# A spiking recurrence and its score matrix: the last step reordered, and three split fetches put back whole

## The chip, the core and the metric

The kernel runs on one core of a Trainium2 chip. The metric is the device time of one execution in microseconds (us); less is better. The core has TensorE (PE in the profile, with its weight loads as PEld), VectorE (DVE), ScalarE (ACT), GpSimd (POOL) and SyncE (SP), a main on-chip memory (SBUF), accumulators (PSUM, eight banks) and 16 DMA engines that move data between them and the chip's memory.

## The reference

B = 1024 sequences of T = 50 item numbers pick rows of a table of N = 100001 items with D = 128 values (row 0 counts as zero). Running means over the sequence are normalised over the batch and drive a leaky neuron per sequence and value; the mean number of its spikes is multiplied with the whole table.

```
e = emb[seq]                                   # (1024, 50, 128)
prefix = jnp.cumsum(e, axis=1)
uF = prefix / minimum(t_idx, lengths)
y = (uF - mean) * rsqrt(var + eps) * gamma + beta   # mean, var over the batch, for each step
for each of the 50 steps t:
    v = v + (y[t] - v) / 2
    spike = v >= 1
    v = v - spike
uF_out = mean of the spikes over the steps     # (1024, 128)
scores = uF_out @ emb.T                        # (1024, 100001), float32
```

The result is 409.6 MB, the table 51 MB.

## The kernel before, in words

The kernel has two stages, and its order of instructions on each engine is the order of the code (`manual_schedule`); waits between engines follow from the tiles that they read and write.

**First stage: the recurrence.** At the start SP fetches the first 40 blocks of the table (a block is 1024 items, `HALF`; 98 blocks in all) into SBUF as rows. Then come 50 steps in the loop over `t`. For each step GpSimd gathers 8 times 128 table rows by an indirect DMA (L218, tile `e`, pool `gp` with two buffers), two steps ahead. TensorE transposes each 128 x 128 piece and adds it to the running sums in PSUM (`pre[0]` and `pre[1]`, one bank each, L332). VectorE divides by the lengths (`uF`, L341, in two halves), takes the statistics (L342, L348), ScalarE and VectorE make the scale `a`, ScalarE writes the scaled input (`x`, L382) into a PSUM tile `vt` (tags `v0` and `v1` in turn), and VectorE adds minus half of `negv` (`step`, L385). `spiked` (L311) adds the spikes of v to `count`; `over` (L304) lets ScalarE write v - 1 as bfloat16 into `d`; `rest` (L308) makes `negv` = spike - v of it, for the next step.

**The last step** (t = 49) is cut so that the second stage can begin early. Its columns go in three pieces: A (128 sequences), B (512) and C (384). Before the sums of this step, VectorE runs `spiked` and `rest` on all 1024 columns of the last v, and makes `near` of A's columns. A is finished on VectorE alone (`vA`, `countA`). PE fills its idle time with 16 transposes of the identity into a tile `warm` (L417) that lies in the bank pair `v0`, where the last v is. Then TensorE multiplies the first two blocks of the table with `countA` (`firsts`: two tiles `po0`, `po1`, each in two halves of 512), and ScalarE (three) and VectorE (one) evict the halves, scaled by 1/T, into `o0` (in a gather tile, tag `e`) and `o1` (tag `rlen` in pool `once`), each half stored by itself (`first_store`, L433 and L435). `x`, `step` and `spiked` of B and C stand between them.

**Second stage: the product.** For each block of the table TensorE transposes the rows, ScalarE and VectorE split the result into two parts (`prepare`, L163 and L164), and TensorE multiplies both parts with the eight groups of counts (`product`, L171) into PSUM tiles of two banks (pool `psum`, four tiles, where the first stage's banks were). The blocks go in groups of `WIDTHS`: four groups of 2, four of 3, thirteen of 6. For each group, and each n of 8 groups of sequences, the blocks' PSUM tiles are evicted by VectorE (L513) and ScalarE (L515) in turn, as `turn` is even or odd, into one output tile, which SP stores in one DMA (`store`, L180): 3 MB for a group of 6. In the groups of 2 there are four output tiles, in a pool that takes the place in SBUF which `once` and the other first-stage pools had; later there are three. The pools are opened with `reuse_waits="tile"`: a new tile waits for what used its place.

**Fetches in the second stage.** From the ninth group on, two times in a group, ScalarE's queue fetches three more blocks (`fetch`, L106 to L139) in one DMA. For the blocks q = 43, 61 and 79 (`LOW`) this is split: the third of the three blocks is fetched by three DMAs of 123, 3 and 2 rows of 4 KB (L116), ahead of one DMA for the other two blocks (L120). Each DMA, of SP and of ScalarE, is given one of eight semaphores in turn, and a DMA on a semaphore is issued when the one before it on that semaphore has landed.

Of the kernel before, what the change touches and what calls it, by code (L numbers as in the profile page):

```python
# [35 lines left out]
NARROW, MIDDLE = 4, 8  # L36
LOW = (43, 61, 79)


@with_exitstack  # L40
def rec_kernel(
# [62 lines left out]
    def fetch(r, k, q, n):  # L104
# [3 lines left out]
        whole = n - (size(q + n - 1) < HALF)  # L108
        if q in LOW:
            whole -= 1  # L110
            n = whole
            one = r[:, k + whole, :]
            src = table[(q + whole) * HALF : (q + whole + 1) * HALF, :].rearrange("(p k) d -> p (k d)", k=KQ)
            p0 = 0
            for pw in (123, 3, 2):
                engine.dma_start(out=one[p0 : p0 + pw, :], in_=src[p0 : p0 + pw, :])  # L116
                p0 += pw
            assert p0 == P
        if whole:
# [63 lines left out]
    with ExitStack() as ph:  # L183
# [122 lines left out]

        def rest(d, v):
            nc.vector.scalar_tensor_tensor(negv, d, 0.0, v, ALU.is_ge, ALU.subtract)  # L308

        def spiked(out, cs, v):  # L310
            nc.vector.scalar_tensor_tensor(out, v, V_TH, count[:, cs], ALU.is_ge, ALU.add)  # L311

        whole = slice(0, B)
        halves = [slice(h * BANK, (h + 1) * BANK) for h in range(B // BANK)]
        v = None

# [3 lines left out]
        for t in range(T):  # L320
            last = t == T - 1
            e = es.pop(t)
            if last:
                spiked(count, whole, v)
                rest(d, v)
                near = once.tile([P, P], F32, tag="r0", name="near")
                nc.vector.tensor_scalar(near, negv[:, :P], -0.5, hgb[:, 1:2], ALU.mult, ALU.add)
            uF = up.tile([P, B], F32, tag="uF", name=f"uF_{t}")
            bs = sp.tile([P, B // BANK, 6], F32, tag="bs", name=f"bs_{t}")
            for h, cs in enumerate(halves):  # L330
                for k in range(0, BANK, P):
# [7 lines left out]
                        skip_group_check=True,  # L339
                    )  # L340
                nc.vector.scalar_tensor_tensor(uF[:, cs], rlen[:, cs], 1.0 / (t + 1), pre[h], ALU.max, ALU.mult)  # L341
                nc.vector.bn_stats(bs[:, h, :], uF[:, cs])  # L342
# [19 lines left out]
            if t and not last:  # L362
                rest(d, v)

# [16 lines left out]
            def x(vt, cs):  # L381
                nc.scalar.activation(vt, uF[:, cs], AF.Identity, bias=hgb[:, 1:2], scale=a)  # L382
# [4 lines left out]
            if not last:  # L387
# [4 lines left out]
                step(vt, whole)  # L392
                v = vt
                d = over(t, v)
                if t + 2 < T:
# [18 lines left out]

        warm = vp.tile([P, HALF], F32, tag="v0", name="warm")
        for k in range(2 * KQ):
            nc.tensor.transpose(warm[:, k % KQ * P : (k % KQ + 1) * P], ident, ident)  # L417
        vC = vp.tile([P, B - BANK - P], F32, tag="v1", name="vC")
        groups = [(slice(P, P + BANK), pre[1], countB), (slice(P + BANK, B), vC, countC)]
        for cs, vt, _ in groups:  # L420
            nc.scalar.activation(uF[:, cs], uF[:, cs], AF.Identity, bias=mv[:, 0:1], scale=-1.0)

        po0 = accp.tile([P, HALF], F32, tag="po0", name="po_0_0")
        po1 = vp.tile([P, HALF], F32, tag="v0", name="po_0_1")
        o0 = gp.tile([P, HALF], F32, tag="e", name="o_0_0")
        o1 = once.tile([P, HALF], F32, tag="rlen", name="o_0_1")
        firsts = [(q, po, o, h, cs) for q, po, o in ((0, po0, o0), (1, po1, o1)) for h, cs in enumerate(halves)]
# [9 lines left out]

        for k, (cs, vt, _) in enumerate(groups):
            x(vt, cs)
            first_store(*firsts[k])  # L440
        for cs, vt, c in groups:
            step(vt, cs)
            spiked(c, cs, vt)
        for f in firsts[2:]:
            first_store(*f)


# [5 lines left out]
    opening = ExitStack()  # L453
    turn = 0
    blocks = 0
# [99 lines left out]
```

## Time and profile before

| What | us |
|---|---|
| Median of three runs (1578.18 to 1581.87) | 1579.38 |
| The profiled execution, its own time | 1581.87 |
| Its span, first to last instruction | 1579.7 |
| v of step 48 done (L385) | 503.54 |
| First product with `countA` starts | 512.16 |
| First store is issued | 514.87 |
| Last store is issued | 1561.73 |

| Engine | busy us | share of the span |
|---|---|---|
| PE | 1111.3 | 70% |
| PEld | 785.6 | 50% |
| DVE | 945.9 | 60% |
| ACT | 667.3 | 42% |
| POOL | 381.0 | 24% |

A line of the timeline has the start, the time busy, the engine, the line, the operation, the tile written and the tiles read, their shapes, and in brackets how long the engine was idle before and what released it. A line of waits has the engine that waited, for whom, the sum in us, how often, and the longest. A line of a table by stretch has the stretch, its length, the busy time of PE, PEld, DVE, ACT and POOL with the number of instructions, the granted share of TensorE's clock, the mean busy share of the 16 DMA engines, and GB/s. The granted clock's first record in this profile is at 465.03 us; ahead of it the column prints full clock.

### The profile page before, as it was taken

What the parts mean: (1) busy time and instruction counts of PE and PEld (TensorE: products, weight loads), DVE (VectorE), ACT (ScalarE), POOL (GpSimd) and SP (SyncE); (2) the same over time, 40 slices, a digit from 0 to 9 for tenths busy, and PEclk for the clock granted to TensorE, in tenths of its full rate; (3) what the DMA queues carried; (4) which work ended last, traced back from release to release, by engine and by line L of the source; (5) the groups of instructions that cost most, each with busy time, mean ns of one, the idle gap of its engine ahead of it and who ended that gap; (6) DMA issues with size and microseconds to landing.
All of it is one profiled execution on the core that took longest, in us unless ns stands there. A gap on an engine that the chain in (4) does not pass through costs nothing.

```text
span 1579.7 us, 12244 instructions
## 1 busy us (share of the span) xinstructions
PE 1111.3 (70%) x4452; PEld 785.6 (50%) x4452; DVE 945.9 (60%) x1125; ACT 667.3 (42%) x697; POOL 381.0 (24%) x406
## 2 busy tenths in 40 slices
PE   4544444444445988899887778886887868888884
PEld 2211111111122766667666566665666656666663
DVE  5777777777777656566555455554555545555552
ACT  2333333333333544555444344443444434444542
POOL 7777777777776000000000000000000000000000
PEclk9999999999995999999999999998999989999998
DMA  9711111111121899999999999998999999999998
GB/s 349 260 53 52 53 52 53 53 53 53 51 80 43 357 415 403 424 414 382 430 425 431 393 426 430 428 430 359 429 427 428 430 366 424 430 429 429 429 427 358
DMA packets 51337, 488.12 MB, mean 309 GB/s; under 512 B 10103, under 2 KB 10360, under 8 KB 30028
## 3 DMA queue, kind: packets, MB, share of 16 engines
q1 hardware_dynamic: 30752, 430.86, 64.7%
q0 software_dynamic: 12800, 26.24, 5.6%
q10 hardware_dynamic: 7724, 30.23, 5.0%
q8 instruction: 35, 0.57, 0.1%
q14 instruction: 26, 0.21, 0.0%
HBM read 77.69 MB, written 409.60 MB: 308 GB/s over the span
## 4 chain that ended last, share of the span: by engine, by line
DMA 53%; POOL 18%; PE 12%; issue 8%; ACT 5%; DVE 2%; ACTq 0%; SPq 0%; DVEq 0%; POOLq 0%
DMA scores<-o 43%; POOL e L218 18%; PE po L171 11%; DMA e<-in_L_rec_emb_table,idx 6%; ACT o L515 4%; DMA rows<-in_L_rec_emb_table 4%; DVE o L513 1%; PE pt L147 0%; ACT pairs L163 0%; PE pre L332 0%; DMA idx<-in_r_seq 0%; DVE pairs L164 0%; DVE negv L308 0%; DVE bs L342 0%; DVE uF L341 0%
## 5 line engine op out<-in xcount | busy, mean ns | idle before, releaser
L513 DVE TENSOR_SCALAR o<-po 128x1024 f32<-128x1024 f32 x391 | 464.1, 1221 | 358.4 <-DMA scores<-o 309.2
L515 ACT ACTIVATE o<-po 128x1024 f32<-128x1024 f32 (+1 forms) x391 | 389.1, 1019 | 551.9 <-DMA scores<-o 330.2
L218 POOL DMA_INDIRECT e<-in_L_rec_emb_table,idx x400 | 380.3, 951 | 123.8 <-issue 112.5
L332 PE MATMUL pre<-ident,e 128*128 128x128 f32 x400 | 179.6, 463 | 230.0 <-DMA e<-in_L_rec_emb_table,idx 229.8
L171 PE MATMUL po<-pairs,countB 128*128 128x512 f32 (+1 forms) x1120 | 289.0, 403 | 64.6 <-ACT o L515 51.7
L171 PE MATMUL po<-pairs,countC 128*128 128x512 f32 (+1 forms) x840 | 227.9, 418 | 62.4 <-ACT o L515 62.4
L171 PEld LDWEIGHTS po<-pairs,countB 128*128 128x128 f32 x1120 | 207.7, 191 | 126.8 <-ACT o L515 68.3
L332 PEld LDWEIGHTS pre<-ident,e 128*128 128x128 f32 x400 | 73.5, 184 | 339.3 <-DMA e<-in_L_rec_emb_table,idx 338.3
L171 PEld LDWEIGHTS po<-pairs,countC 128*128 128x128 f32 x840 | 163.3, 201 | 108.5 <-ACT o L515 74.2
L164 DVE TENSOR_TENSOR pairs<-pt,pairs 128x1024 fp32r<-128x1024 f32 x70 | 84.6, 1216 | 84.0 <-ACT pairs L163 84.0
L341 DVE SCALAR_TENSOR_TENSOR uF<-rlen,pre 128x512 f32<-128x512 f32 x100 | 68.3, 683 | 109.4 <-PE pre L332 109.4
L147 PE MATMUL pt<-ident,rows 128*128 128x128 f32 (+1 forms) x768 | 104.6, 281 | 10.3 <-issue 4.9
L352 ACT ACTIVATE r<-mv,eps 128x1 f32<-128x1 f32 x50 | 14.7, 295 | 225.4 <-DVE mv L348 225.4
L147 PEld LDWEIGHTS pt<-ident,rows 128*128 128x128 f32 (+1 forms) x768 | 93.5, 146 | 27.0 <-issue 10.3
L171 PE MATMUL po<-hi,countB 128*128 128x512 f32 x208 | 84.7, 407 | 16.0 <-ACT o L515 12.0
L292 PE MATMUL pre<-zT,ls 128*128 128x512 f32 x100 | 78.1, 783 | 22.7 <-DVE uF L341 18.8
L171 PE MATMUL po<-lo,countB 128*128 128x512 f32 x208 | 81.8, 393 | 0.0
L304 ACT ACTIVATE d<-v,less 128x1024 bf16<-128x1024 f32 x49 | 54.6, 1114 | 63.6 <-DVE v L385 63.6
L171 PE MATMUL po<-hi,countC 128*128 128x512 f32 x156 | 65.5, 420 | 21.8 <-ACT o L515 21.7
L163 ACT CAST pairs<-pt 128x1024 fp32r<-128x1024 f32 x70 | 70.5, 1007 | 12.6 <-PE pt L147 12.6
L171 PE MATMUL po<-pairs,countA 128*128 128x512 f32 x280 | 69.3, 394 | 7.3 <-ACT o L515 7.3
L382 ACT ACTIVATE v<-uF,hgb,a 128x1024 f32<-128x1024 f32 x49 | 59.2, 1208 | 30.6 <-DVE a L378 30.5
(85 smaller groups left out, 847.1 us busy)
## 6 DMA issues: line engine op xcount, KB each, us to landing
scores<-o SPq DMA_DIRECT2D x96, 3072.0 KB, 19.7
scores<-o SPq DMA_DIRECT2D x32, 1536.0 KB, 8.7
scores<-o SPq DMA_DIRECT2D x30, 1024.0 KB, 8.6
rows<-in_L_rec_emb_table ACTq DMA_DIRECT2D x16, 1536.0 KB, 29.6
scores<-o SPq DMA_DIRECT2D x8, 2896.5 KB, 17.6
rows<-in_L_rec_emb_table SPq DMA_DIRECT2D x5, 3072.0 KB, 32.7
e<-in_L_rec_emb_table,idx POOLq DMA_INDIRECT x400, 2.5
rows<-in_L_rec_emb_table ACTq DMA_DIRECT2D x3, 1024.0 KB, 33.6
```

The costliest lines, as they stand in the source:

```text
L147: nc.tensor.transpose(pt[:, k0 : k0 + pw], r[:pw, k0 : k0 + D], ident[:pw, :pw])
L163: nc.scalar.copy(vh, vp)
L164: nc.vector.tensor_tensor(vl, vp, vh.bitcast(F32), ALU.subtract)
L171: nc.tensor.matmul(po[:, :kw], lhsT=counts[n], rhs=part[:, k0 : k0 + kw], start=j == 0, stop=j == 1,)
L218: nc.gpsimd.indirect_dma_start(out=es[t][:, n * P : (n + 1) * P], out_offset=None, in_=table, in_offset=bass.IndirectOffsetOnAxis(ap=idx[: ...
L292: nc.tensor.matmul(pre[h], lhsT=l, rhs=zT[:, h * BANK : (h + 1) * BANK], start=t == 0, stop=False, skip_group_check=True,)
L304: nc.scalar.activation(d, v, AF.Identity, bias=less)
L332: nc.tensor.matmul(pre[h][:, k : k + P], lhsT=e[:, h * BANK + k : h * BANK + k + P], rhs=ident, start=False, stop=last, is_transpose=True, ...
L341: nc.vector.scalar_tensor_tensor(uF[:, cs], rlen[:, cs], 1.0 / (t + 1), pre[h], ALU.max, ALU.mult)
L382: nc.scalar.activation(vt, uF[:, cs], AF.Identity, bias=hgb[:, 1:2], scale=a)
L513: nc.vector.tensor_scalar_mul(o[:, h0 : h0 + hw], po[:, :hw], 1.0 / T)
L515: nc.scalar.mul(o[:, h0 : h0 + hw], po[:, :hw], 1.0 / T)
```

## The change

The change has three parts.

- **The last step.** `spiked` on all of v moves from the start of the last step to the end of the one before, between `step` and `over`, that is ahead of ScalarE's copy `d`. `rest` takes a slice of columns: the last step's start does only A's 128; B's and C's come later, around B's `step`. TensorE transposes the identity four times after each of the first three gathered pieces of the second half, and 16 times `near` behind the last; all of these go to the tile `warm`, which now lies in the bank pair of `po0`.
- **The first block's outputs.** `o1` is in the second gather tile (tag `e`) instead of `rlen`. `po1` is in `v1`, and C's v in `v0`. All four evictions of `firsts` come ahead of C's `x`, `step` and `spiked`. The second stage's `turn` starts at 1, so that its first eviction is ScalarE's.
- **The fetches.** `LOW` is gone: all fetches of three blocks are one DMA.

```diff
-LOW = (43, 61, 79)
...
         whole = n - (size(q + n - 1) < HALF)
-        if q in LOW:
-            whole -= 1
-            n = whole
-            one = r[:, k + whole, :]
-            src = table[(q + whole) * HALF : (q + whole + 1) * HALF, :].rearrange("(p k) d -> p (k d)", k=KQ)
-            p0 = 0
-            for pw in (123, 3, 2):
-                engine.dma_start(out=one[p0 : p0 + pw, :], in_=src[p0 : p0 + pw, :])
-                p0 += pw
-            assert p0 == P
...
-        def rest(d, v):
-            nc.vector.scalar_tensor_tensor(negv, d, 0.0, v, ALU.is_ge, ALU.subtract)
+        def rest(d, v, cs):
+            nc.vector.scalar_tensor_tensor(negv[:, cs], d[:, cs], 0.0, v[:, cs], ALU.is_ge, ALU.subtract)
...
+        pieceA, pieceB, pieceC = slice(0, P), slice(P, P + BANK), slice(P + BANK, B)
+        warm = accp.tile([P, HALF], F32, tag="po0", name="warm")
+
+        def keep_busy(tile, times):
+            for k in range(times):
+                nc.tensor.transpose(warm[:, k % KQ * P : (k % KQ + 1) * P], tile, ident)
...
             if last:
-                spiked(count, whole, v)
-                rest(d, v)
+                rest(d, v, pieceA)
...
+                    if last and h and k + P < BANK:
+                        keep_busy(ident, KQ // 2)
...
             if t and not last:
-                rest(d, v)
+                rest(d, v, whole)
...
                 step(vt, whole)
                 v = vt
+                if t == T - 2:
+                    spiked(count, whole, v)
                 d = over(t, v)
...
-        warm = vp.tile([P, HALF], F32, tag="v0", name="warm")
-        for k in range(2 * KQ):
-            nc.tensor.transpose(warm[:, k % KQ * P : (k % KQ + 1) * P], ident, ident)
-        vC = vp.tile([P, B - BANK - P], F32, tag="v1", name="vC")
-        groups = [(slice(P, P + BANK), pre[1], countB), (slice(P + BANK, B), vC, countC)]
-        for cs, vt, _ in groups:
+        keep_busy(near, 2 * KQ)
+        for cs in (pieceB, pieceC):
             nc.scalar.activation(uF[:, cs], uF[:, cs], AF.Identity, bias=mv[:, 0:1], scale=-1.0)
...
-        po1 = vp.tile([P, HALF], F32, tag="v0", name="po_0_1")
+        po1 = vp.tile([P, HALF], F32, tag="v1", name="po_0_1")
         o0 = gp.tile([P, HALF], F32, tag="e", name="o_0_0")
-        o1 = once.tile([P, HALF], F32, tag="rlen", name="o_0_1")
+        o1 = gp.tile([P, HALF], F32, tag="e", name="o_0_1")
...
-        for k, (cs, vt, _) in enumerate(groups):
-            x(vt, cs)
-            first_store(*firsts[k])
-        for cs, vt, c in groups:
-            step(vt, cs)
-            spiked(c, cs, vt)
-        for f in firsts[2:]:
+        x(pre[1], pieceB)
+        rest(d, v, pieceB)
+        step(pre[1], pieceB)
+        spiked(countB, pieceB, pre[1])
+        rest(d, v, pieceC)
+        for f in firsts:
             first_store(*f)
+        vC = vp.tile([P, B - BANK - P], F32, tag="v0", name="vC")
+        x(vC, pieceC)
+        step(vC, pieceC)
+        spiked(countC, pieceC, vC)
...
-    turn = 0
+    turn = 1
```

## The prediction

> **What bounds the kernel now.** I read the page first: slices, chain, issues. It shows two stages. Up to 513 us the steps run at the pace of the gathers; after that DMA is full at 425 to 430 GB/s, except in some slices.
>
> ```profile
> DMA  9711111111121899999999999998999999999998
> GB/s 349 260 53 52 53 52 53 53 53 53 51 80 43 357 415 403 424 414 382 430 425 431 393 426 430 428 430 359 429 427 428 430 366 424 430 429 429 429 427 358
> DMA 53%; POOL 18%; PE 12%; issue 8%; ACT 5%; DVE 2%; ACTq 0%; SPq 0%; DVEq 0%; POOLq 0%
> ```
>
> A slice is 39.5 us. The dips to 393, 359 and 366 stand at 870, 1070 and 1270. The table by stretch gives their depth, the waits of SP's queue after 730 us their cause:
>
> ```profile
> 870.00:880.00 10.00, 8.87 (x48) 7.17 (x47) 5.86 (x5) 5.29 (x6) 0.00 (x0) 1.00 0.94 304
> 1070.00:1085.00 15.00, 12.91 (x56) 10.54 (x57) 8.80 (x8) 7.86 (x8) 0.00 (x0) 0.89 0.68 242
> 1100.00:1250.00 150.00, 122.08 (x560) 96.70 (x559) 80.31 (x69) 68.01 (x69) 0.00 (x0) 0.98 1.00 427
> 1275.00:1289.00 14.00, 12.33 (x54) 10.08 (x55) 8.25 (x7) 7.86 (x8) 0.00 (x0) 0.88 0.73 256
> ```
> ```profile
> SPq L180 <- DVE o L513: 658.5, 94, 15.2
> SPq L180 <- DMA rows<-in_L_rec_emb_table: 71.2, 3, 24.6
> SPq L180 <- ACT o L515: 66.5, 88, 1.7
> ```
>
> The last two columns of the table are DMA share and GB/s. Three times a store that is otherwise due is held, up to 24.6 us, by a fetch; there are 19 fetches, and three of them are the LOW ones. The DMA issues show why: a LOW fetch is four DMAs on four of the eight DMA semaphores (847 us: 104, 105, 107, 117), and the store issued at 878.15 uses 104 again. It had to wait for the 123 rows.
>
> Then the last step and the first stores, in the timeline, and PE's clock by stretch (third column from the end):
>
> ```profile
> 503.57 1.11 ACT L304 ACTIVATE d<-v,less 128x1024 bf16<-128x1024 f32 x1 [1.30 <-DVE v L385]
> 504.72 1.23 DVE L311 SCALAR_TENSOR_TENSOR count<-v,count 128x1024 bf16<-128x1024 f32 x1 [1.18 <-ACT d L304]
> 505.86 1.21 DVE L308 SCALAR_TENSOR_TENSOR negv<-d,v 128x1024 f32<-128x1024 bf16 x1
> 507.31 0.68 DVE L341 SCALAR_TENSOR_TENSOR uF<-rlen,pre 128x512 f32<-128x512 f32 x1
> 512.16 0.77 PE L171 MATMUL po<-hi,countA 128*128 128x512 f32 x1 [1.31 <-DVE a L374]
> 514.25 0.60 ACT L435 ACTIVATE o<-po 128x512 f32<-128x512 f32 x1 [1.26 <-PE po L171]
> 519.55 3.67 DVE L513 TENSOR_SCALAR o<-po 128x1024 f32<-128x1024 f32 x3 [2.27 <-PE po L171]
> ```
> ```profile
> 461.62:465.03 3.41, 3.01 (x13) 2.64 (x13) 1.39 (x2) 2.11 (x3) 2.50 (x4) 1.00 0.29 61
> 465.03:468.44 3.41, 0.66 (x2) 0.28 (x2) 2.51 (x3) 0.23 (x1) 2.49 (x4) 1.00 0.90 326
> 512.79:516.23 3.44, 3.44 (x10) 2.67 (x9) 2.14 (x4) 2.15 (x5) 0.00 (x0) 0.50 0.14 54
> 519.00:521.30 2.30, 1.86 (x8) 1.24 (x7) 1.75 (x2) 1.62 (x2) 0.00 (x0) 1.00 0.00 0
> ```
>
> DVE idles 1.18 us before the count, the first products run at half clock (one per 0.43 us, against 0.23 after 516.2), and DMA stands still from 519.0 to 521.3, after stores of only 256 KB: the chain there is the store at 517.30, its 2.12 us to landing, then ACT at 519.68. The evictions of block n=1 wait for that landing, although their products ended at 517.05: their output tile lies where o_0_1 (tag rlen) was.
>
> **The change, part 1: the last step (before the first store).** Count directly behind v fills DVE's idle 1.18 us. Before, the count waited for ACT's copy of the same tile; I take it that the copy now waits for the count, so d ends at 505.95 instead of 504.68. Then rest on 128 columns (as `near`, 0.29, instead of 1.21) and near 0.29: uF starts at 506.65 instead of 507.31, a gain of 0.65. If the two don't wait for each other, the last transpose (506.96 to 507.43) is late next, and the gain is 1.2. The rest of B and C (about 0.68 and 0.56, by L385's rows) moves behind `a`: B's beside ACT's x (0.78), C's ahead of the DVE eviction, which still comes 2 us sooner than now.
>
> PE: 4 idle transposes after each of three gathered ones are 5 x 0.226 = 1.13 us of work in the gathers' 1.25 us, so they delay nothing; 16 more run from 507.45 to 511.1 at most, and the products are due at 511.5. Thus PE is nearly without a gap from 503.3 on, and the clock should rise before 511. The row for it is the stretch 461.62 to 465.03: 13 transposes, 3.01 us of 3.41 busy, and full clock right after, until 468.44. (The clock's records begin at 465.03, so the 1.00 printed for the stretch itself means nothing; a lone transpose takes 0.47 us before it, 0.33 at 465.39 and 0.47 again at 469.50.) In today's last step no whole 3.41 us stretch is so filled, and the clock rises at 516.23. With the clock, product 4 ends at 511.5 + 3 x 0.227 + 0.4 = 512.6 instead of 514.21, and the first store leaves at 513.2, not 514.87: 1.65 us sooner. Without it, 0.65.
>
> The Trainium skill speaks against this: "TensorE: Matmul & The Clock Gate", Part 4 (PE-mode transpose), says that transposes don't count as PE activity and the full clock doesn't engage for them. By that page the idle transposes would bring nothing, and the gain up to the effective start would be about 1 us; the row at 465.03 contradicts it, and I go by the row.
>
> **Part 2: the first outputs.** With o_0_1 in the second gather tile, n=1 waits for no landing. ACT: three evictions from 512.6 (0.60 each), x of C 0.67, to 515.1; B counted at 513.8; n=1's first product 513.8 to 514.9, evicted by ACT (hence turn = 1) at 516.1 against 520.7. The second waits, at worst, for C's count at 516.3: stored at 517.5 to 518.6 (521.23 now), and n=2 at 518.8 to 519.9 (521.97 now). From packet shares, DMA has done 3.0 us of full work by 522.0 today: an effective start at 519.0. Then: four stores of 256 KB and two of 512 KB are 5.1 us of work by 520.3 to 521.4, so 515.2 to 516.3. Gain 2.7 to 3.7; I take **3.2**; without the clock about 1. Everything behind is a full DMA, so it carries to the end. The swap of ACT and DVE in 391 evictions (1.02 against 1.22) lies beside DMA and is put at nothing; the last store is issued 16 us before DMA ends. Where evictions set the pace it would cost 0.2 us per store.
>
> **Part 3: no LOW.** Bytes stay the same. The trace's packet records have no engine, but on one engine a packet starts 3 or 4 ns before the previous one ends, so sixteen lanes can be followed. They show three engines with the LOW rows (124 to 127 reads against 108 to 111 from 885 to 1070), and another one that is slow: 940 ns per 24 KB packet against 919 (1480 to the end), 936 against 912 to 916 earlier. That slow engine ends last, at 1578.36; a second at 1577.38; the other fourteen between 1571.8 and 1574.6. So the end is set by the slow engine's own work. Two terms for it:
> - more: 3 blocks x 8 rows x 0.16 us = +3.8.
> - less: its pauses in the three holds. From its last packet to the restart it has 4.35, 7.25 and 7.95 us (874.7 to 879.05, 1076.8 to 1084.05, 1280.6 to 1288.55), and in each it reads 24 rows that it must read anyway (3.84): 0.5 + 3.4 + 4.1 = -8.0.
>
> Sum **-4.2**. The other engines lose 20 us in the holds (3.9, 8.5, 7.9), but they are ahead of it. Bounds: +3.8 if the slow engine loses nothing now, -16.5 (20.3 less 3.8) if it is no brake.
>
> The page "DMA: Bandwidth & Descriptors", Latency and other measured facts, calls engines 7 and 15 usually slower and guesses at the rings of software DMA as a cause. By that the slow lane should be gone after the last gather, and the sum would be the -16.5; the lane is slow to the end, with no software packet after 513, so I stay with the first.
>
> **Sum.** 3.2 + 4.2 = 7.4. The profiled execution took 1581.87 (span 1579.7, 2.2 around it): 1574.5. The median of the three runs is 2.5 lower, 1579.38: **1572.0**.
>
> **The rivals.**
> - The slow engine is no brake (another share of it in unprofiled runs, or fast engines set the pace): 3.2 + about 12, taking most of the 15.3 us that the missing bytes of the dips make at 429 GB/s. 1564. For it: fourteen engines are done 4 to 7 us early; against it: the last lane. 0.24.
> - The pauses cost the slow engine nothing, only the 3.8 us stay: -3.2 + 3.8, 1580: no change. For it: it reads through much of each pause. 0.14.
> - Slower: without pauses its lag grows by 2.4%. Three output tiles allow a lead of some 9 us (two stores of 7.3 less 6 for evicting and issuing), reached after 360 us, at about 1090. From there the fast engines wait at each store and read in bursts, and reads go at 0.20 and not 0.16 us, as they do in today's pauses (57 reads in 11.4 us). 15 fetches x 24 rows x 0.04 = +14.4: 1586. It decides if all reads fall into bursts; against it, a wait of 0.2 us per store is no burst. 0.06.
> - The clock doesn't rise: within the forecast's case, 1574.2.
>
> **How the numbers follow.** Forecast 0.56, in its own range 1567 to 1576. 0.2% is 3.2 us, about what a measurement of this kernel can tell from no change; faster then means below 1576.2. The forecast's case and the first rival give 0.80 faster, with 0.14 within and 0.06 slower. Range 1562.5 to 1577.5: it leaves out most of the last two rivals.
>
> **What would show it.** SP's waits name no fetch after 730, and slices at 870, 1070, 1270 read 425 to 430; full clock before the first product; first store about 513.2; no DMA gap at 519; n=1 evicted by 516.5; one lane still last. I am wrong if DMA dips elsewhere at the output tiles, if the first store leaves after 514, or if the last lane ends later after the start than now.

## The result, and the profile after

The kernel after took 1576.07 us (median of 14 runs, 1574.12 to 1577.66) beside 1578.95 for the kernel before (14 runs) on the same chip: a ratio of 0.9978 with a 95% interval of 0.9970 to 0.9986, that is 2.2 to 4.7 us less. The forecast was 7.4 us less. The sign was right and the time lies in the range, but well over half of the expected gain is missing. The profiled execution of after took 1576.4 us (span 1574.6).

One thing is needed to read the sizes: the runs of the kernel before fall into two groups, 11 of these 14 between 1577.7 and 1579.4 and three between 1581.9 and 1582.4, and the profiled one (1581.87) is in the upper group.

First the slices and SP's waits after 730 us, in the profile of after:

```profile
DMA  9711111111121899999999999999999999999998
GB/s 347 264 52 54 52 54 52 53 53 54 52 79 47 337 414 414 423 413 402 428 427 429 427 426 421 421 409 429 421 428 424 402 428 429 414 423 417 426 405 354
```
```profile
SPq L169 <- DVE o L511: 794.7, 103, 14.1
SPq L549 <- DMA scores<-o: 16.2, 3, 6.9
```

No store waits for a fetch any more, and the three deep dips (393, 359, 366) are gone. There are new shallow ones: 409, 402, 414, 417. The stretches of the old holds and two early stretches:

```profile
870.00:880.00 10.00, 8.47 (x46) 6.88 (x45) 5.80 (x5) 5.05 (x6) 0.00 (x0) 1.00 1.02 433
1070.00:1085.00 15.00, 14.01 (x61) 11.40 (x62) 9.50 (x8) 7.83 (x8) 0.00 (x0) 0.89 0.99 421
1275.00:1289.00 14.00, 12.70 (x59) 9.90 (x58) 7.63 (x7) 5.92 (x7) 0.00 (x0) 0.94 1.02 437
516.00:522.00 6.00, 5.66 (x25) 4.73 (x26) 3.47 (x4) 2.15 (x3) 0.00 (x0) 1.00 0.69 275
534.00:542.00 8.00, 7.81 (x26) 5.74 (x25) 3.74 (x4) 3.08 (x3) 0.00 (x0) 0.66 0.66 270
```

The first three rows are what part 3 was to bring. The last is new: from 534 to 542 DMA is busy only 0.66 of the time and PE's clock is at 0.66. In the kernel before, DMA was full there and the clock stayed up from 516 to 717. The timeline of the last step of after:

```profile
503.72 1.23 DVE L300 SCALAR_TENSOR_TENSOR count<-v,count 128x1024 bf16<-128x1024 f32 x1
504.98 1.11 ACT L293 ACTIVATE d<-v,less 128x1024 bf16<-128x1024 f32 x1 [2.56 <-DVE count L300]
506.65 0.68 DVE L338 SCALAR_TENSOR_TENSOR uF<-rlen,pre 128x512 f32<-128x512 f32 x1
507.28 2.61 PE L309 MATMUL warm<-ident,near 128*128 128x128 f32 x16
511.50 0.47 PE L160 MATMUL po<-hi,countA 128*128 128x512 f32 x1 [1.61 <-DVE a L371]
511.81 0.40 PE L160 MATMUL po<-lo,countA 128*128 128x512 f32 x1
512.70 1.58 ACT L430 ACTIVATE o<-po 128x512 f32<-128x512 f32 x3 [0.37 <-PE po L160]
513.32 7.66 SPq L169 DMA_DIRECT2D scores<-o  x7
515.07 1.02 ACT L513 ACTIVATE o<-po 128x1024 f32<-128x1024 f32 x1
516.34 0.47 PE L160 MATMUL po<-hi,countB 128*128 128x512 f32 x1 [1.31 <-DVE countC L300]
```
```profile
508.70:512.00 3.30, 1.69 (x13) 1.44 (x12) 3.09 (x11) 1.87 (x4) 0.00 (x0) 1.00 0.00 0
```

ACT's copy `d` waits for the count (v is done at 503.68, `d` starts 1.30 us later), `uF` starts at 506.65, the first product at 511.50 at full clock (its record rises from 0.5 to 1.0 at 508.71), the first store at 513.32, and block n=1 is evicted from 515.07: each within 0.15 us of its forecast. The gain up to here is real; it is lost behind it.

### The profile page after: what moved, and what is told of

It is laid out like the page before. It is cut to its first block, busy times and chain, and to the rows that moved or that the text cites. A ratio compares the mean times of both kernels' runs of the same rounds, so it can differ in the third digit from the quotient of the medians.

```text
span 1574.6 us, 12255 instructions
## 1 busy us (share of the span) xinstructions
PE 1128.4 (72%) x4464; PEld 799.5 (51%) x4464; DVE 949.3 (60%) x1127; ACT 673.4 (43%) x697; POOL 380.9 (24%) x406
## 4 chain that ended last, share of the span: by engine, by line
DMA 48%; POOL 18%; PE 15%; issue 8%; DVE 5%; ACT 4%; ACTq 0%; SPq 0%; POOLq 0%; DVEq 0%
DMA scores<-o 42%; POOL e L207 18%; PE po L160 14%; DMA e<-in_L_rec_emb_table,idx 6%; DVE o L511 3%; ACT o L513 3%; DVE pairs L153 1%; ACT pairs L152 0%; PE pt L136 0%; ACT hi L152 0%; DVE lo L153 0%; PE pre L327 0%; DMA idx<-in_r_seq 0%; DVE bs L339 0%; DVE uF L338 0%
## 5 line engine op out<-in xcount | busy, mean ns | idle before, releaser
L511 DVE TENSOR_SCALAR o<-po 128x1024 f32<-128x1024 f32 (+1 forms) x391 | 467.3, 1214 | 329.5 <-DMA scores<-o 187.4
L513 ACT ACTIVATE o<-po 128x1024 f32<-128x1024 f32 x391 | 392.0, 1025 | 506.0 <-DMA scores<-o 362.7
L160 PE MATMUL po<-pairs,countB 128*128 128x512 f32 (+1 forms) x1120 | 292.8, 408 | 57.8 <-ACT o L513 57.8
L160 PE MATMUL po<-pairs,countC 128*128 128x512 f32 (+1 forms) x840 | 240.1, 433 | 59.4 <-ACT o L513 53.4
L160 PEld LDWEIGHTS po<-pairs,countB 128*128 128x128 f32 x1120 | 211.8, 194 | 119.2 <-ACT o L513 76.7
L160 PEld LDWEIGHTS po<-pairs,countC 128*128 128x128 f32 x840 | 168.1, 208 | 112.1 <-ACT o L513 65.5
L281 PE MATMUL pre<-zT,ls 128*128 128x512 f32 x100 | 77.5, 777 | 23.2 <-DVE uF L338 19.3
L339 DVE BATCH_NORM_STATS2 bs<-uF 128x6 f32<-128x512 f32 x100 | 69.4, 694 | 3.5
## 6 DMA issues: line engine op xcount, KB each, us to landing
rows<-in_L_rec_emb_table ACTq DMA_DIRECT2D x19, 1536.0 KB, 29.3
```

The lines of the kernel that those rows point to most:

```text
L160: nc.tensor.matmul(po[:, :kw], lhsT=counts[n], rhs=part[:, k0 : k0 + kw], start=j == 0, stop=j == 1,)
L281: nc.tensor.matmul(pre[h], lhsT=l, rhs=zT[:, h * BANK : (h + 1) * BANK], start=t == 0, stop=False, skip_group_check=True,)
L511: nc.vector.tensor_scalar_mul(o[:, h0 : h0 + hw], po[:, :hw], 1.0 / T)
L513: nc.scalar.mul(o[:, h0 : h0 + hw], po[:, :hw], 1.0 / T)
```

## The experiments

The runs come from three chips of the same kind besides the first. On one of them (called the slow chip here: e1 to e8) the 50 steps take some 60 us longer, with gaps of some 6 us on GpSimd, and the times of one kernel spread over 10 us. Ratios of that chip tell parts of 0.2% apart, no less. To read smaller things there I use traces, with the time counted from the end of v of step 48 or from the first store. On the other chips (e9 to e12, and e13 and e14) a kernel without `LOW` repeats within 1 to 3 us.

| Kernel | median us | before, same chip | ratio (95%) |
|---|---|---|---|
| e1, before without `LOW` | 1642.12 | 1645.18 | 0.9970 (0.9951 to 0.9989) |
| e2, after with `LOW` | 1645.72 | 1645.18 | 0.9997 (0.9981 to 1.0014) |
| e3, after, turn = 0 | 1640.70 | 1645.18 | 0.9972 (0.9954 to 0.9991) |
| e4, `LOW` split evenly | 1641.70 | 1645.18 | 0.9973 (0.9955 to 0.9992) |
| e5, e3 with eight blocks 119 + 9 | 1652.99 | 1645.75 | 1.0046 (1.0026 to 1.0065) |
| e6, e1 with turn = 1 | 1642.52 | 1645.75 | 0.9980 (0.9964 to 0.9997) |
| e7, e3 without idle transposes | 1642.87 | 1645.75 | 0.9984 (0.9970 to 0.9999) |
| e8, e3 with `o1` in `rlen` | 1642.56 | 1645.75 | 0.9981 (0.9966 to 0.9995) |
| e10, before without `LOW` | 1576.49 | 1579.06 | 0.9980 (0.9971 to 0.9989) |
| e11, after | 1575.63 | 1579.06 | 0.9978 (0.9969 to 0.9987) |
| e12, after, turn = 0 | 1573.97 | 1579.06 | 0.9969 (0.9957 to 0.9982) |
| e13, e12 with four blocks 4 + 124 | 1570.05 | 1578.26 | 0.9949 (0.9936 to 0.9963) |
| e14, before, `LOW` 4 + 124, last | 1572.64 | 1578.26 | 0.9968 (0.9956 to 0.9980) |

**e1: part 3 alone.**

```diff
-LOW = (43, 61, 79)
+LOW = ()
```

> The kernel before with LOW empty: part 3 alone. Theory A (the three holds of SP are what LOW costs, and the first-stage gain is given back at 530 to 542 us where PE falls to half clock): 2.5 to 4.5 us faster than before, no wait of SP for a fetch after 730 us. Theory B (the slow DMA engine's own work is the end and it loses nothing in the holds; the earlier start carries through): 0 to 4 us slower than before.

Ratio 0.9970, and SP's waits name no fetch. Within the intervals, part 3 alone brings as much as the whole change did on the first chip.

**e2: parts 1 and 2 alone** (the kernel after with `LOW` and its split kept).

> The changed kernel with the LOW fetches kept: parts 1 and 2 alone. Theory A: first 2 MB of scores out about 3 us earlier than before, but level with it at 10 MB (0.0 to 0.3 us), and the time within 1 us of before. Theory B: the start stays 2.5 to 3.5 us ahead and the time is 2.5 to 3.5 us below before.

Ratio 0.9997: nothing that can be measured. Its waits after 730 us show the three holds again:

```profile
SPq L180 <- DVE o L522: 779.6, 112, 16.6
SPq L180 <- DMA rows<-in_L_rec_emb_table: 67.3, 3, 24.3
```

So of the start gain of parts 1 and 2 nothing reaches the end that this chip's interval would show. PE's clock falls to 0.5 here too, from 22.2 to 25.6 us behind the first store (19.3 to 26.1 in after).

**e3: the order of the evicting engines** (the kernel after).

```diff
-    turn = 1
+    turn = 0
```

> The changed kernel with turn starting at 0, so that VectorE and ScalarE change places in all 391 evictions. Theory A, if the stall at 529 to 532 us comes from this order (ScalarE evicts and then casts twice in a row while PE waits): no half clock at 532 to 539, no DMA share of 0.66 at 534 to 542, and the start gain carries: 2 to 3 us faster than the changed kernel, about 5.5 below before. If the order is not the cause: the same time as the changed kernel within 1 us. Theory B says nothing is lost there: the same within 1 us.

No drop of the clock after the first stores, and the start gain stands up to 80 MB of scores. The total, 0.9972, can't be told from e1's on this chip; e10 to e12 repeat the three on a steadier one.

**e4: the same four DMAs, evenly loaded.**

```diff
-            for pw in (123, 3, 2):
+            for pw in (64, 32, 32):
```

> The kernel before with the third block of a LOW fetch split into 64, 32 and 32 rows instead of 123, 3 and 2: still four DMAs on four semaphores, but every engine gets its 8 rows. Theory A (three engines with 43 rows land late and hold the store): the holds vanish, time as with LOW empty within 1 us. Rival (four semaphores taken at once are what holds SP, whatever they carry): holds of 10 us and more stay, time as before within 1 us.

Ratio 0.9973, no wait for a fetch, as without `LOW`. Four DMAs on four semaphores make no hold; the uneven load is what made them.

**e5: which engine is slow** (e3, and for eight blocks `for p0, p1 in ((0, 119), (119, P))` in the place of `LOW`'s loop).

> The kernel after with turn = 0, and for eight blocks (43, 49, 55, 61, 67, 73, 79, 85) the third block of the fetch is read by two DMAs of 119 and 9 rows, ahead of the DMA of the other two. By the read counts of the LOW lanes (123 rows lay on three engines, 84 rows on fourteen) I expect 119 rows to go to seven engines, 17 each, and 9 rows to nine, one each; so the engines outside the seven read 7 or 8 rows less a block. Theory A (one slow engine, 940 ns a packet against 919, sets the pace of the whole second stage; the others wait for it at the output tiles): if it is outside the seven, it reads 56 to 64 rows of 0.16 us less, 9.0 to 10.2 us, and the kernel is 7 to 10 us faster than without the splits: ratio to the kernel before 0.991 to 0.993, the last lane still alone but the others nearer to it. If it is inside the seven, it reads 80 rows more: 12.8 us slower, ratio 1.005. The rival (the end is set by evictions or by all engines alike): all sixteen engines read the same bytes in sum, so the time stays within 2 us of the one without splits (0.9972 of before in an earlier comparison), or is longer where a fetch holds a store.

Slower, 10 us more than e7 and e8 on the same chip, beside a term of 12.8. The lanes of the first split and the next fetch (902 to 978 us) settle the place: seven lanes have 57 or 58 reads, nine have 40 or 41, and the one whose 24 KB packets take 928 ns against 912 has 58. The slow engine is one of the seven. (The records name no engine. The lanes are followed from packet to packet as in the prediction, and where two of them change packets in the same nanosecond the choice is open.) It is not the only thing that the split did: seven stores were held by a fetch, 67.4 us in sum, so the 10 us are not all the engine's.

**e6: turn = 1 alone** (e1 with `turn = 1`).

> The kernel before with LOW = () and turn = 1: of part 2 only the order of the evicting engines. Theory B (with turn = 1 ScalarE's eviction and its two casts come one behind the other at the start of the second stage, PE waits and loses its clock, and DMA starves for some us): PE's clock drops to 0.5 within 45 us behind the last gather, and 10 MB are stored 1.0 to 2.8 us later after the first store than with turn = 0; the total is 0 to 3 us longer than that of LOW = () alone: ratio 0.997 to 0.999. The rival (the drop needs the new last step as well, or the earlier stores): no drop of the clock, 10 MB at the same time as in the kernel before within 0.3 us, ratio 0.997.

The rival was right: no drop, and 10 MB come 0.1 us earlier after the first store than in the kernel before. Two casts stand in a row here too, and PE waits, but less (0.76 and 1.07 us), and its clock stays up:

```profile
600.00:602.00 2.00, 1.18 (x5) 0.67 (x4) 1.85 (x2) 1.13 (x2) 0.00 (x0) 1.00 0.98 401
602.00:604.00 2.00, 0.93 (x4) 0.48 (x3) 1.64 (x2) 1.02 (x1) 0.00 (x0) 1.00 1.01 418
```

So in this trace the wrong parity by itself loses nothing at the start; the ratio (0.9964 to 0.9997) can't tell it from e1's. It costs together with the new start.

**e7: the idle transposes** (e3, `for k in range(0)` in `keep_busy`).

> The kernel after with turn = 0 and without the idle transposes of the last step. My theory (they raise PE's clock): without them the clock is at 0.5 during the first products, a product takes 0.43 us and not 0.23, and the first store is issued 0.8 to 1.2 us later behind v of step 48 than the 9.8 us of the kernel after where the gathers set the pace. The rival (transposes don't count for the clock): the clock and the first store are as with them. In the total either is 1 us at most, less than the comparison can tell: ratio 0.996 to 0.998.

From the end of v of step 48 to the first product it takes 7.83 us (7.82 in after, 8.62 in before); from there to the first store 2.70 us (1.82 in after, 2.71 in before). The first products in e7:

```profile
579.78 0.77 PE L160 MATMUL po<-hi,countA 128*128 128x512 f32 x1 [10.71 <-DVE a L371]
580.34 0.63 PE L160 MATMUL po<-lo,countA 128*128 128x512 f32 x1
580.77 0.63 PE L160 MATMUL po<-hi,countA 128*128 128x512 f32 x1
```

One product per 0.43 us, where after has one per 0.23. But e3, which differs from e7 only by its idle transposes, took the same 2.70 us: its step 48 ran late behind a gap, the gathered pieces had all landed, PE stood idle 3.4 us before the 16 transposes of `near`, and the first products ran at half clock in spite of the idle transposes. So e7 beside e3 does not price them. What shows that transposes raise the clock is after's own trace: from 503.29 to 511.50 PE runs nothing but transposes, and the clock's record rises at 508.71. The Trainium skill's rule ("TensorE: Matmul & The Clock Gate", Part 4 (PE-mode transpose)), that transposes do not engage the full clock, does not hold here.

The full clock is worth 0.88 us up to the first store. It came in time in six of the nine profiles with the new idle transposes: in after, e8, e9, e11, e12 and e13 (1.82 to 1.84 us from first product to first store), but not in e2, e3 and e5, all on the slow chip (2.70 to 2.71). In e2 the clock had risen and fallen again before the products. With the 16 transposes of the old last step it came in time once in six, in e14 (1.83), and not in before, e1, e4, e6 and e10. That once looks like chance: the records change in steps of 3.41 us, and in e14 one such stretch (507.04 to 510.45) lay wholly within transposes, where in the kernel before the stretch from 505.96 to 509.37 holds a gap of 0.78 us and the next one the wait for `countA`.

**e8: `o1` back in `rlen`** (e3).

```diff
-        o1 = gp.tile([P, HALF], F32, tag="e", name="o_0_1")
+        o1 = once.tile([P, HALF], F32, tag="rlen", name="o_0_1")
```

> The kernel after with turn = 0, and o_0_1 back in the tile rlen. My theory (part 2's term: the evictions of block n = 1 wait for the landing of the store of o_0_1): DMA stands still for 1.5 to 2.5 us some 4 to 6 us after the first store, 2 MB are out 1.2 to 2.0 us later after the first store than without this edit. If start gains carry to the end, the total is 1 to 2 us longer than with turn = 0 alone (0.9972 of before): ratio 0.998; if they are levelled at the next change of pools (80 to 90 MB), 90 MB come at the same time as in the kernel with turn = 0 alone and the ratio is 0.997.

The gap of DMA is back, and with it the wait for a landing of VectorE's first eviction of n=1:

```profile
586.66:588.66 2.00, 2.00 (x6) 1.61 (x5) 1.23 (x1) 1.02 (x1) 0.00 (x0) 0.50 0.00 0
```
```profile
586.95 1.23 DVE L511 TENSOR_SCALAR o<-po 128x1024 f32<-128x1024 f32 x1 [1.43 <-DMA scores<-o]
```

Counted from the first store, 2 MB are out 0.4 us earlier than in the kernel before (e3: 1.5, e7: 1.3), 80 MB 0.1 later (e3 1.0 earlier, e7 0.9). That puts the new place of `o1` at 1.1 us. But in e8 the clock was up before the first products and in e3 and e7 it was not; beside e12, where it was up too (2 MB 1.9 earlier, 80 MB 1.5 earlier), it is worth 1.5. The ratio does not resolve it.

**e9: the slow engine's place, closer** (e12, three blocks split 114 + 14, 115 + 13 and 124 + 4).

> The kernel after with turn = 0, and for three blocks the third block of the fetch is read by two DMAs: block 43 by 114 and 14 rows, block 61 by 115 and 13, block 79 by 124 and 4. The earlier split of 119 rows lay on seven engines, and the slow engine was one of them (58 reads of 4 KB, as the six others, against 40 or 41); it was none of the three engines of the 123 rows. So it is one of the fourth to seventh engine. By the same rule 114 rows lie on six engines (19 each), 115 on five (23), 124 on four (31), always the first. Expected, from the read counts of the lane whose 24 KB packets take longest: few reads in the first split means that it is the seventh, few in the second the sixth or seventh, few in the third any but the fourth. The rival to one slow engine at a fixed place (a lane that is slow for what it happens to carry): the slow lane falls in no consistent place, for instance among the many readers in the third split and the few in the second but not the first. The time is for reading only: within 5 us of turn = 0 alone.

On another chip than e5, and a single execution (1576.91 us). In the first split six lanes have 58 to 60 reads, and the slow one (931 ns) is one of them. In the second it has 54 and reads on to 1111, as the four with 63 or 64 do, while the others end between 1095 and 1102. In the third it is done at 16 reads, as the light ones, while the heavy ones are at 23 to 30 and still reading. With the nesting that the counts suggest (each split takes the first so many engines) that is the fifth engine. The Trainium skill's page "DMA: Bandwidth & Descriptors", Latency and other measured facts, names engines 7 and 15 as usually slower; by these counts it is neither here.

**e10, e11, e12: the parts on a steady chip** (e1, after and e3 again, in one comparison).

> The kernel before with LOW = (), a second time, on the same chip as the kernel after and its turn = 0, so that parts 1 and 2 can be priced on top of part 3. Theory A (the holds are all that LOW cost): ratio to the kernel before 0.997, as before (0.9970), that is 4 to 5 us less.

> The kernel after itself. Theory B (its earlier first stores are given back between 16 and 28 us after the first store, where ScalarE's eviction and two casts come one behind the other): within 1 us of LOW = () alone on the same chip. The rival (start gains are kept, 3 us): 2.5 to 3.5 us faster than LOW = () alone, a ratio to it of 0.998.

> The kernel after with turn = 0. Theory B: no drop of PE's clock at 25 to 40 us behind the last gather, 10 MB out about 1 us sooner after the first store than in the kernel before; 1.5 to 2.5 us faster than LOW = () alone (0.8 us from v to the first product, up to 0.9 from there to the first store where the clock is up, 0.9 behind it), a ratio to it of 0.9985 to 0.999, and as much faster than the kernel after. The rival (the slow engine's lane levels all gains of the start): no difference of the three.

Without `LOW` 1576.49 (11 runs, 1576.15 to 1577.28), after 1575.63 (11 runs, 1574.49 to 1577.45), turn = 0 1573.97 (6 runs: five from 1573.62 to 1574.09, one of 1575.89). Part 3 brings 2.6 us by the medians, less than the expected 4 to 5. On top of it, parts 1 and 2 bring 0.86 us with turn = 1 and 2.52 with turn = 0. From the traces, the time from the first store until so much of the scores is out, less that of the kernel before, in us; the first row is the time from the end of v of step 48 to the first store, likewise:

| | e10 | e11 (after) | e12 (turn = 0) |
|---|---|---|---|
| to the first store (before: 11.33) | 0.0 | -1.7 | -1.7 |
| 2 MB | 0.0 | -1.8 | -1.9 |
| 10 MB | 0.0 | +1.8 | -1.4 |
| 80 MB | 0.0 | +1.4 | -1.5 |
| 90 MB | -1.6 | -0.6 | -3.1 |
| end of DMA | -4.9 | -3.9 | -6.5 |

The first row and a later one add up: with turn = 0 the scores are 3.1 us ahead from 10 to 80 MB, with turn = 1 not at all. (What e10 gains between 80 and 90 MB is taken up under part 3 below.) Between 2 and 10 MB after loses 3.6 us, 3.0 more than turn = 0. ScalarE, VectorE and PE there, and the same time by stretches, first in after (e11), then with turn = 0 (e12):

```profile
528.87 1.02 ACT L513 ACTIVATE o<-po 128x1024 f32<-128x1024 f32 x1 [1.48 <-PE po L160]
529.79 1.93 ACT L152 CAST hi<-pt 128x1024 fp32r<-128x1024 f32 x2
530.83 1.23 DVE L153 TENSOR_TENSOR lo<-pt,hi 128x1024 fp32r<-128x1024 f32 x1 [3.22 <-ACT hi L152]
530.85 0.50 PE L160 MATMUL po<-hi,countA 128*128 128x512 f32 x1 [1.19 <-ACT hi L152]
532.11 0.50 PE L160 MATMUL po<-lo,countA 128*128 128x512 f32 x1 [0.76 <-DVE lo L153]
534.37 0.80 PE L160 MATMUL po<-lo,countA 128*128 128x512 f32 x1 [0.77 <-DVE lo L153]
```
```profile
529.00:532.00 3.00, 1.16 (x8) 0.61 (x5) 1.17 (x2) 2.71 (x3) 0.00 (x0) 1.00 0.99 412
532.00:535.00 3.00, 2.13 (x6) 1.21 (x7) 2.31 (x3) 1.02 (x1) 0.00 (x0) 0.64 0.81 339
535.00:538.00 3.00, 3.00 (x9) 2.33 (x8) 1.23 (x1) 0.19 (x1) 0.00 (x0) 0.50 0.56 229
```
```profile
528.36 1.01 ACT L152 CAST hi<-pt 128x1024 fp32r<-128x1024 f32 x1 [0.61 <-PE pt L136]
529.34 1.02 ACT L513 ACTIVATE o<-po 128x1024 f32<-128x1024 f32 x1
530.26 1.01 ACT L152 CAST hi<-pt 128x1024 fp32r<-128x1024 f32 x1
530.40 2.35 DVE L153 TENSOR_TENSOR lo<-pt,hi 128x1024 fp32r<-128x1024 f32 x2
530.41 0.49 PE L160 MATMUL po<-hi,countA 128*128 128x512 f32 x1 [0.29 <-ACT o L513]
531.67 0.50 PE L160 MATMUL po<-lo,countA 128*128 128x512 f32 x1 [0.77 <-DVE lo L153]
```
```profile
529.00:532.00 3.00, 1.94 (x12) 1.28 (x10) 2.74 (x3) 2.26 (x3) 0.00 (x0) 1.00 1.01 415
532.00:535.00 3.00, 3.00 (x14) 2.18 (x13) 2.17 (x3) 1.03 (x1) 0.00 (x0) 1.00 0.99 412
535.00:538.00 3.00, 3.00 (x18) 2.56 (x17) 2.18 (x2) 1.52 (x2) 0.00 (x0) 1.00 1.05 434
```

These are the last evictions of the first group, and behind them the splits of the next two blocks. With turn = 0 ScalarE casts the first, then evicts, then casts the second. With turn = 1 it evicts first and then has both casts in a row; VectorE, which must subtract what was cast (3.22 us idle), and PE, which needs the result, stand still. PE is busy 1.16 of 3 us, its clock goes to 0.5, and in the next 6 us it does half the products (9 in 3 us against 18) while DMA runs out of stores (0.56). So turn = 1 costs the start gain; that much the pair shows.

Whether the waits or the clock's drop behind them cost the time is less clear. After, e2 and e11 have the two casts in a row, the drop and the starved DMA. e6 has the casts in a row without the drop, and loses nothing. e14 (below; turn = 0, casts apart) has a drop without the row of casts: PE is busy 1.46 us of 531 to 534, the clock is at 0.5 from 534.3 to 537.8, yet DMA stays at 1.02 and nothing is lost up to 80 MB. The loss came only where both came together with the new, earlier start; no run separates the three. That a drop of the clock alone can cost DMA time shows at another place, under part 3 below.

**e13 and e14: relief for the slow engine, behind the main fetch** (e13: e12 with four blocks; e14: the kernel before with its three `LOW` blocks). In both, the DMA of two blocks is issued first, and then:

```diff
-            for pw in (123, 3, 2):
-                engine.dma_start(out=one[p0 : p0 + pw, :], in_=src[p0 : p0 + pw, :])
-                p0 += pw
+            for p0, p1 in ((124, P), (0, 124)):
+                engine.dma_start(out=one[p0:p1, :], in_=src[p0:p1, :])
```

> The kernel after with turn = 0, and for four blocks (43, 55, 67, 79) the third block is read by two DMAs of 4 and 124 rows behind the DMA of the other two. The 124 rows lie on the first four engines; in the split of 124 rows before, the slow engine was not among the heavy readers, so it reads 8 rows less a block: 4 x 8 x 0.16 = 5.1 us in all, the four read 15.4 us more, less than the some 22 us that the slow engine lags by rate (1042 packets x 21 ns). Since the 124 rows come last, their semaphore comes up again seven stores later (51 us), about when they land (16 + 31 reads of 1.1 us = 52 us after the issue), so holds are 0 to 3 us each. Theory A (the slow engine's own work sets the end): 3.5 to 5 us faster than turn = 0 alone, ratio to the kernel before 0.994 to 0.995 where turn = 0 had 0.9969. The rival (bytes in sum, or evictions, set it): as turn = 0 alone, 0.997, or up to 3 us slower by holds.

> The kernel before, its three LOW blocks kept (43, 61, 79), but read by two DMAs of 4 and 124 rows behind the DMA of the other two, instead of 123, 3 and 2 rows ahead of it. The slow engine is relieved by the same 8 rows a block (3.8 us in all). Theory A (LOW brings 3.8 us on the slow engine and loses more by its holds): SP's waits name fetches for under 10 us instead of 71, and the kernel is 2 to 3.8 us faster than LOW = () alone: ratio to the kernel before 0.9955 to 0.997. The rival (the relief is worth nothing, the slow engine is no brake): as LOW = (), 0.998, or worse by the holds that are left.

e14 takes 1572.64: 5.6 us less than the kernel before beside it, and 3.85 less than e10's 1576.49 on another chip (whose kernel before was 0.8 us slower), against an expected 2 to 3.8; with each counted from its own chip's kernel before it is 3.05. e13 takes 1570.05, 8.2 us less than the kernel before (0.9949); it beats both kernels. It is 3.9 less than e12's 1573.97, or 3.1 counted from each chip's kernel before, against an expected 3.5 to 5 and 5.1 us of reads moved. The traces lie between: from the first store to the end of DMA e14 takes 3.5 us less than e10 and e13 3.7 less than e12. So with three blocks the relief of the slow engine is worth about what its reads cost, with four less than that. In the traces the lane that ends last in after, e10, e11, e12 and e14 has the longer packets to its end (866 to 880 ns for the 23 KB of the last group); in e13 the last packets take 861 ns as on the other lanes, so there the slow engine no longer ends last.

One expectation failed in both: the holds did not go. SP's waits and three stretches around the last holds of e14:

```profile
SPq L179 <- DMA rows<-in_L_rec_emb_table: 63.2, 4, 17.6
```
```profile
918.00:924.00 6.00, 6.00 (x28) 4.96 (x27) 2.54 (x3) 2.14 (x3) 0.00 (x0) 0.83 0.86 352
1118.00:1126.00 8.00, 7.90 (x32) 6.10 (x30) 3.96 (x4) 3.13 (x4) 0.00 (x0) 0.79 0.81 335
1319.00:1327.00 8.00, 7.58 (x30) 6.24 (x31) 3.94 (x4) 2.99 (x4) 0.00 (x0) 0.79 0.72 296
```

SP waits 63 us for fetches, hardly less than the 71 of the kernel before, and e13 even 91. What has changed is what DMA does meanwhile. In e14 the holds leave (1 - 0.86) x 6 + (1 - 0.81) x 8 + (1 - 0.72) x 8 = 4.6 us of DMA unused; in the kernel before, by its three stretches shown ahead, 0.6 + 4.8 + 3.8 = 9.2. And in e14's holds never fewer than five engines are busy, the four that read the 124 rows and one more; in the last two holds of the kernel before only three or four are left for some 3 us. I take the fifth for the slow engine that no longer runs dry. The trace can't be followed lane by lane through these holds, so this last step is argued from the counts and not shown.

## Why the prediction was right or wrong

By the steady chip the missing 4.0 us (7.4 less 3.43, the difference of e11 to its kernel before) come from three places.

**"Everything behind is a full DMA, so it carries to the end", and "the swap of ACT and DVE ... is put at nothing": wrong by 1.7 us.** This is the failed step of the start term. I looked at the swap only as 391 evictions of 1.02 or 1.22 us beside DMA, and not at what else stands on ScalarE's queue when the order is shifted by one: the two casts of the next blocks. e12 less e11 is the price, 1.66 us by the medians (2.5 by the ends of DMA in the two traces, all of it lost before 10 MB). DMA was full behind the start in the kernel before; that does not make it full after a change.

**The start term itself: 3.2 predicted, 2.5 with turn = 0.** The working up to the first store was right: 0.80 us by the reordered count and rest (8.62 to 7.82), where 0.65 was predicted, and 0.88 by the clock (2.71 to 1.82), where 1.0 was, together 1.68 against 1.65. The row at 465 us, from which I took that transposes raise the clock, was the right guide. The effective start of DMA came at 516.25 (2.7 us earlier), the low end of my 2.7 to 3.7. With turn = 0 the traces have 3.1 us from 10 to 80 MB and 3.2 at the end of DMA (e12 less e10), so the term was sized about right, and the 2.5 of the medians may be their spread. "No DMA gap at 519" was a miss: the landing's wait was gone (1.1 to 1.5 us, e8), but the second block of n=1 waited for C's count at 516.34, "at worst" in the prediction, so that DMA was at 0.69 from 516 to 522.

**Part 3: 4.2 predicted, 2.6 measured (e10).** The two terms were +3.8 for the reads that go back to the slow engine and -8.0 for its pauses. By e14 less e10 the first is 3.1 to 3.9 us. The second then is 5.6 to 6.4 by the medians: the pauses were put too high. The miss is not beyond noise, though: e10's interval is 1.7 to 4.6 us.

The pauses were taken from the profiled execution, which was one of the long runs of the kernel before, and "the median of the three runs is 2.5 lower" was taken off both kernels without asking where the 2.5 us arise. The traces show a part of it. The profiled execution of e10 is 4.9 us ahead of that of the kernel before at the end of DMA, but 1.6 of them come between 80 and 90 MB, at the change from groups of 3 to groups of 6 and over 100 us ahead of the first `LOW` fetch (846 us). There, 200 to 210 us behind the first store, the kernel before and then e1, which lacks `LOW`:

```profile
714.87:719.87 5.00, 3.68 (x10) 2.64 (x11) 3.43 (x3) 3.02 (x4) 0.00 (x0) 0.77 0.71 297
719.87:724.87 5.00, 5.00 (x25) 4.17 (x24) 2.50 (x3) 2.53 (x4) 0.00 (x0) 0.88 0.68 285
```
```profile
776.80:781.80 5.00, 3.72 (x15) 2.76 (x16) 3.47 (x4) 3.45 (x4) 0.00 (x0) 1.00 0.71 295
781.80:786.80 5.00, 5.00 (x28) 4.21 (x27) 3.04 (x4) 2.96 (x3) 0.00 (x0) 1.00 0.85 359
```

In the kernel before, PE's clock drops for 3.4 us at 717.6 and DMA falls behind by 1.6 us. e3, without `LOW`, has the same drop at the same place and the same loss; e2, which keeps `LOW`, has neither. So these 1.6 us are not `LOW`'s, and what `LOW` costs in this pair of traces is 3.3 us, where 4.2 was predicted. Whether this drop is what parts the two groups of runs of the kernel before stays open: only one long run was profiled.

The rivals: that the slow engine is no brake is refuted by e13 and e14, which move rows from it to others and gain 3 to 4 us; the last lane still ends 5.3 us behind most others in after (1573.1 against 1567.8). That its pauses cost it nothing is refuted by e1 and e10. Of the slower rival, the lag cap, the trace of after shows the beginning: in five dips of 1.5 to 2.6 us between 1037 and 1505 us the number of busy engines falls to one or two, and I take it that they wait at the output tiles. Its price (+14.4) did not come.

## What to carry to other kernels

When an engine's order shifts by one, go through everything on that engine's queue at the boundaries of stages, not only through the operation whose parity changed: two instructions that now stand in a row can starve PE, and its clock can fall after that (to 0.5 for 6.8 us in after). Before a forecast, look whether the profiled run is a typical one of its kernel: a term read from it is paid only in runs like it, and a second trace of the kernel shows how much of a difference lies outside the change. And when one DMA engine is slower than the others, rows moved off it are worth their time until another engine ends last (three blocks here, not four). Issue the uneven transfer behind the ones that all engines share: ahead of them the same rows cost 2.6 us (`LOW` against e10), behind them they brought 3 to 4 (e14).

## What the runs showed of the hardware

- One DMA engine was 2% slower than the rest for whole kernels (928 to 940 ns per 24 KB packet against 912 to 919), with no software-issued transfer after the first stage. The read counts of the chips where I could locate it fit one place (one of the seven on one, the fifth on another; on a third, e13's gain fits an engine outside the four), but each place rests on one trace.
- Reads of rows spread over fewer engines than 16 when the number of rows doesn't divide: 123 rows on three lanes, 124 on four, 115 on five, 114 on six, 119 on seven.
- A fetch of three blocks is 24 reads of 0.16 us for an engine, 3.8 us, yet it took 29.6 us from issue to landing in the kernel before and 29.3 in e12: the engine's store packets go between the reads (in e9's third split a lane that made 31 reads moved 25 store packets in the same 28 us). So 43 reads on one engine made a store wait far longer than their own 6.9 us (up to 24.6 us here).
- Two reads of one accumulator tile by VectorE and ScalarE went one after the other in both kernels, in the order of the program: in after `d` starts 1.30 us after v, at the end of `count`; in before `count` waits 1.18 us for `d`. No run shows whether the chip would let them overlap.
- PE that ran nothing but transposes from 503.29 on was granted the full clock at 508.71 (after).
- A drop of PE's clock to 0.5 for 3.4 us put the scores 1.6 us back at the change of groups (before and e3, 80 to 90 MB), and in e14, where DMA stayed full, it put them back by nothing.
